# A mixture-of-experts phase in written order, its results turned by VectorE and by way of DRAM

## The chip, the cores and the metric

The kernel runs on one core of one Trainium2 chip. The metric is the device time of one execution in microseconds (us), the median of three runs. A second source is one profiled execution of the same program, whose trace gives start, duration and releaser of every instruction.

## What is computed

Eight sequences of 1024 tokens, 512 features each, pass through one layer in float32. With `xn` the layer-normalised input, the result is `x + s * silu(shared + routed)`:

```python
xn = _layernorm(x)
s = out_h @ W2 + b2                 # a gated linear recurrence over xn, projected
shared_out = _swiglu(xn, shared_gate_w, shared_up_w, shared_down_w)
topk_ids = argmax(xn @ gate_w)      # one of 32 experts for each token
xs = xn * sigmoid(topk_val)
routed_out = (silu(xs @ gate_e) * (xs @ up_e)) @ down_e   # e: the token's expert
```

Each expert has three matrices of 512x1024, 512x1024 and 1024x512, that is 2 MB each. A token goes to exactly one expert.

## The kernel before

**Two phases.** The first phase does all that is dense: normalisation, the recurrence, the shared expert and the router. It leaves in DRAM two tables of records: `rec1` holds each token's scaled input `xs`, `rec2` holds three rows for each token, its `x`, its recurrent output without the bias `b2`, and its shared output. Its instructions are issued in an order written out by hand (`tc.manual_schedule()`, closed by `order.close()`, L1397). The second phase runs over the 32 experts; here the scheduler of the framework is free to order the instructions of each engine.

**One expert.** The tokens of an expert are a chunk. Chunks are sorted by size and get fixed widths W, from 376 tokens for the first down to 224 for the last two (`WIDTHS`). A chunk of over 256 tokens has three tiles of up to 128 tokens, the others two: 20 chunks with three and 12 with two make 84 tiles. (Tokens beyond a chunk's width would go to an overflow loop at the end, L1431, which has no turn in this data.)

- `weights` (L195) loads the three matrices on SP's DMA queue into seven rotating buffers, so that a load waits for the expert that used its buffer two experts earlier.
- `gather_in` (L199) fetches `xs` on POOL's queue, 32 tokens to a DMA, so that `transpose` (L228) can turn them by VectorE in 32x32 blocks to `xsT`, with features on the partitions. The first chunk alone is fetched in whole rows and turned by TensorE.
- `gather_rest` (L218) fetches the records of `rec2`, on POOL too.
- `compute` (L252) has eight steps j. In each, TensorE multiplies gate and up (`g`, `u`, eight instructions, L272), ScalarE takes the sigmoid (L277), VectorE makes `h` (L279, L280), and TensorE multiplies the `h` of the step before by the down matrix into four PSUM tiles `acc` (L261). The trace shows each such instruction as two matmuls. So `h` of step j is wanted only after `g` and `u` of step j+1. A float32 expert is 192 pairs of weight load and matmul.
- At the end ScalarE copies the four `acc` to `yT` (L289). They hold the result with features on the partitions.
- `finish` (L291), a tile at a time and in the steps 1, 2 and 3 of the next expert, adds `b2` to the record (L297), turns `yT` back by four TensorE transposes into a PSUM tile `tb` (L300), adds the shared output (L304), takes silu with ScalarE's sigmoid (L306, L307), multiplies by the recurrent output (L308), adds `x` (L309) and scatters the rows to the output on POOL's queue (L310).

**Work between the steps.** `compute` takes a table `between` of what is issued after step j (L1412 to L1419): `finish` of the expert before, `transpose` of the next one from step 4 on, and after step 6 the weights and inputs of the expert after that. Where an instruction stands in an engine's queue is then up to the scheduler.

Of the kernel before, what the change touches and what calls it, by code (L numbers as in the profile page):

```python
# [8 lines left out]
FP = mybir.dt.float32  # L9
# [8 lines left out]
P = 128  # L18
T = 512
NT = T // P  # L20
BL = 32
# [12 lines left out]
def tile_kernel(  # L34
# [73 lines left out]
    def work(name):  # L108
        return pools["work"].tile([P, 512], FP, tag="w", name=name)
# [53 lines left out]
    def expert(where):  # L163
        e = nc.values_load(
            where, engines=[ET.SP], min_val=0, max_val=E - 1,
            skip_runtime_bounds_check_because="the numbers of experts, or a count of them, clamped",
        )
        return [w[bass.ds(e, 1)].rearrange("o a b -> (o a) b") for w in (rgate_w, rup_w, rdown_w)]

    class Chunk:  # L170
# [3 lines left out]

        def __init__(self, alloc, alloc_w, name, cols, fours, width, w_src, whole=False):
            self.whole = whole
            self.alloc, self.alloc_w, self.name, self.w_src = alloc, alloc_w, name, w_src
            self.width, self.cols, self.fours = width, cols, fours  # L180
            self.wt, self.src = [], None
            self.tiles = [
                (t, min(P, width - t * P)) for t in range(-(-width // P))
            ]
# [67 lines left out]
        def compute(self, between):  # L252


            wg, wu, wd = self.wt
            xsT, alloc, name, W = self.xsT, self.alloc, self.name, self.width
            accs = [pools["acc"].tile([P, H], FP, tag="acc", name=f"{name}_acc{m}") for m in range(KH)]

            def down(j, h):
                for m in range(KH):  # L260
                    nc.tensor.matmul(  # L261
                        accs[m][:, :W], lhsT=wd[:, j, m * P : (m + 1) * P], rhs=h[:, :W],
                        start=(j == 0), stop=(j == NI - 1),
                    )

            last = None
            for j in range(NI):
                g = work(f"{name}_g{j}")
                u = work(f"{name}_u{j}")
                for o, w in ((g, wg), (u, wu)):  # L270
                    for k in range(KH):
                        nc.tensor.matmul(  # L272
                            o[:, :W], lhsT=w[:, k, j * P : (j + 1) * P], rhs=xsT[:, k, :W],
                            start=(k == 0), stop=(k == KH - 1),
                        )
                sig = alloc([P, C], "sig", f"{name}_sig{j}")
                nc.scalar.activation(sig[:, :W], g[:, :W], AF.Sigmoid)  # L277
                h = alloc([P, C], "h", f"{name}_h{j}")
                nc.vector.tensor_tensor(sig[:, :W], sig[:, :W], g[:, :W], ALU.mult)  # L279
                nc.vector.tensor_tensor(h[:, :W], sig[:, :W], u[:, :W], ALU.mult)  # L280
                if last is not None:
                    down(*last)
                last = (j, h)
                for step in between.get(j, ()):
                    step()
            down(*last)
            self.yT = alloc([P, KH, C], "yT", f"{name}_yT")
            for m in range(KH):
                nc.scalar.copy(self.yT[:, m, :W], accs[m][:, :W])  # L289

        def finish(self, t):  # L291

            if t >= len(self.tiles):
                return
            n, col = self.tiles[t][1], self.cols(t)
            name, alloc, r = self.name, self.alloc, self.rest[t]
            nc.vector.tensor_tensor(r[:n, H : 2 * H], r[:n, H : 2 * H], b2b[:n, :], ALU.add)  # L297
            ps = work(f"{name}_tb{t}")
            for m in range(KH):
                nc.tensor.transpose(  # L300
                    ps[:n, m * P : (m + 1) * P], self.yT[:, m, t * P : t * P + n], ident
                )
            z = alloc([P, H], "z", f"{name}_z{t}")
            nc.vector.tensor_tensor(z[:n, :], ps[:n, :], r[:n, 2 * H :], ALU.add)  # L304
            s = alloc([P, H], "s", f"{name}_s{t}")
            nc.scalar.activation(s[:n, :], z[:n, :], AF.Sigmoid)  # L306
            nc.vector.tensor_tensor(z[:n, :], z[:n, :], s[:n, :], ALU.mult)  # L307
            nc.vector.tensor_tensor(z[:n, :], z[:n, :], r[:n, H : 2 * H], ALU.mult)  # L308
            nc.vector.tensor_tensor(z[:n, :], z[:n, :], r[:n, :H], ALU.add)  # L309
            nc.gpsimd.indirect_dma_start(  # L310
                out=of[:, :], out_offset=bass.IndirectOffsetOnAxis(ap=col[:n, :], axis=0),
                in_=z[:n, :], in_offset=None, bounds_check=N - 1, oob_is_err=False,
            )


    NW = 7
    turn = iter(range(3 * E))

# [2 lines left out]
        return pools["wa" if i < 4 else "wb"].tile(shape, FP, tag=f"w{i}", name=name)  # L321

    def alloc2(shape, tag, name):
        bufs = {"xs": 2 * CT, "xsT": 2, "sig": 2, "h": 3, "z": 3, "s": 2, "yT": 2, "rest": CT + 1}
        pool = pools["in" if tag in ("xs", "xsT") else "by"]
        return pool.tile(shape, FP, tag=tag, name=name, bufs=bufs[tag])

# [2 lines left out]
            alloc2, alloc_w, f"e{e}",  # L330
            lambda t, e=e: pools["idx"][:, e * CT + t : e * CT + t + 1],
            lambda t, b, e=e: pools["fours"][:, b, e * CT + t : e * CT + t + 1],
            WIDTHS[e], lambda e=e: expert(eid[0:1, e : e + 1]), e == 0,
        )
        for e in range(E)
    ]
# [44 lines left out]
    class Prep:  # L381
# [40 lines left out]
        def store(self, t):  # L422
            i = (self.c * NT + t) * P
            nc.sync.dma_start(out=xnd[i : i + P, :], in_=self.xs[t])
# [173 lines left out]
    def fetch(n):  # L598
        sum_tile(n)
        nc.sync.dma_start(  # L600
            out=sums[n].rearrange("p s k f -> p (s k f)"), in_=sdram[n % JC][:, :]
        )
# [38 lines left out]
    def bias(n, block):  # L641
        p, kind = JOBS[n % JC]
        col = "hfi".index(kind) * NJ + 2 * p + block
        return vec[:, col : col + 1]
# [749 lines left out]
    pools["work"] = ps_w  # L1394
    for t in range(CT):
        chunks[0].transpose(t)
    order.close()  # L1397
    c1.close()


    pools["acc"] = ctx.enter_context(
        tc.tile_pool(name="ps_acc", bufs=4, space=PSUM, reuse_waits="tile")
    )
    with ExitStack() as c3:
        pools["wb"] = c3.enter_context(tc.tile_pool(name="wb", bufs=1, reuse_waits="tile"))
        pools["by"] = c3.enter_context(tc.tile_pool(name="by", bufs=2, reuse_waits="tile"))
        chunks[1].weights()
        for e, chunk in enumerate(chunks):
            chunk.gather_rest()
            if e == 0:  # L1410
                chunks[1].gather_in()
            between = {j: [] for j in range(NI)}  # L1412
            for t in range(CT):
                if e:
                    between[1 + t].append(lambda t=t: chunks[e - 1].finish(t))
                if e + 1 < E:
                    between[4 + t].append(lambda t=t: chunks[e + 1].transpose(t))
            if e + 2 < E:
                between[6] += [chunks[e + 2].weights, chunks[e + 2].gather_in]  # L1419
            chunk.compute(between)  # L1420
        for t in range(CT):
            chunks[-1].finish(t)
    c2.close()


    with tc.tile_pool(name="wo", bufs=3) as wo, tc.tile_pool(name="so", bufs=3) as so:
        n = nc.values_load(  # L1427
            nov[0:1, 0:1], min_val=0, max_val=MAXOV,
            skip_runtime_bounds_check_because="a sum of at most MAXOV comparisons of counts that sum to N",
        )  # L1430
        with tc.For_i(0, n, 1) as i:  # L1431
            ci = so.tile([P, CT], I32, tag="ci", name="ci")
            nc.vector.tensor_copy(ci, pools["idx"][:, bass.ds(i * CT + E * CT, CT)])
            cf = so.tile([P, NA, CT], I32, tag="cf", name="cf")
            nc.vector.tensor_copy(cf, pools["fours"][:, :, bass.ds(i * CT + E * CT, CT)])

            def alloc(shape, tag, name):
                return so.tile(shape, FP, tag=tag, name=name)

            chunk = Chunk(  # L1440
                alloc, lambda shape, name: wo.tile(shape, FP, tag="w", name=name), "ov",
                lambda t: ci[:, t : t + 1], lambda t, b: cf[:, b, t : t + 1], C,
                lambda: expert(ovexp[0:1, bass.ds(i, 1)]),
            )
            chunk.weights()
            chunk.gather_in()
            chunk.gather_rest()
            for t in range(CT):
                chunk.transpose(t)
            chunk.compute({})  # L1450
            for t in range(CT):
                chunk.finish(t)


# [30 lines left out]
```

## Time and profile before

| | us |
|---|---|
| median of 3 runs (4343.04 to 4348.74) | 4345.41 |
| the profiled execution | 4345.11 |
| its span, first to last instruction | 4343.3 |
| first matmul of the second phase after the span's start | 2848.26 |
| end of the last expert's down matmuls, about | 4321.6 |
| TensorE busy with matmuls in between | 1467.82 of 1473.34 |
| VectorE busy there | 553.71 |
| ScalarE busy there | 203.56 |

The profile's page gives busy time by engine and groups of instructions by line. "PE" is TensorE's matmul, "PEld" its weight load, "DVE" VectorE, "ACT" ScalarE, "POOL" GpSimd, "SP" the queue that issues most DMAs. In a timeline each row has the start, the busy time and the engine of some instructions, their line and tiles, how many they are, and in brackets how long the engine stood idle before and who ended it. The recorded end of a matmul is modelled, since matmuls are pipelined: the time that one takes from its successor is read from start to start.

### The profile page before, as it was taken

The numbers are of one execution on the slowest core, as the hardware profiler recorded it, in microseconds if no ns is written. First come the engines' busy times: TensorE is split into PE (matmuls) and PEld (weight loads), VectorE is DVE, ScalarE is ACT, GpSimd is POOL, SyncE is SP. The second block draws the span as 40 slices with busy tenths as digits, with TensorE's granted clock in tenths as the row PEclk, the third lists the DMA queues.
The fourth block names the chain that finished last, engine by engine and source line by source line (L and its number), as shares of the span: only waits on it lengthen the run. The fifth ranks groups of instructions, "written<-read, shape, count | busy, mean of one in ns | idle before, by whom it ended". The sixth has DMA issues, their size and how long they took to land. (4 is left out here: it accounts for less than half of the span.)

```text
span 4343.3 us, 52479 instructions
## 1 busy us (share of the span) xinstructions
PE 4262.1 (98%) x19031; PEld 3560.0 (82%) x19031; DVE 2761.5 (64%) x3507; ACT 1661.3 (38%) x3319; POOL 1748.4 (40%) x1410
## 2 busy tenths in 40 slices
PE   8899999999999999999999999999999999999998
PEld 3488888888888888888888888866777788889998
DVE  6787877886977778778878788723334334343332
ACT  3355555555555555555555544401111111111111
POOL 4445444534453444445434536642222233332210
PEclk9999999999999999999999999999999999999999
DMA  7667676676666666766766655574555555565561
GB/s 245 204 213 225 213 222 208 207 230 206 212 213 223 219 209 209 224 202 214 223 217 214 209 187 169 183 255 165 185 185 183 177 213 201 197 230 204 205 230 63
DMA packets 459433, 889.58 MB, mean 205 GB/s; under 512 B 35167, under 2 KB 285823, under 8 KB 450980
## 3 DMA queue, kind: packets, MB, share of 16 engines
q1 hardware_dynamic: 431588, 796.22, 55.1%
q0 software_dynamic: 27584, 89.98, 6.5%
q8 instruction: 152, 2.49, 0.2%
q14 instruction: 109, 0.89, 0.1%
HBM read 787.64 MB, written 116.50 MB: 208 GB/s over the span
## 5 line engine op out<-in xcount | busy, mean ns | idle before, releaser
L694 PE MATMUL b<-t,sums 128*128 128x256 f32 x2400 | 618.9, 380 | 8.6 <-DVE t L626 6.3
L981 PE MATMUL u<-wP,s 128*128 128x256 f32 x2048 | 601.9, 381 | 2.4 <-DMA wP<-tdram 2.4
L261 PE MATMUL e_acc<-e_h,e_wd 128*128 128x296 f32 (+15 forms) x2048 | 515.4, 397 | 5.5 <-DVE e_h L280 5.5
L272 PE MATMUL e_g<-e_xsT,e_wg 128*128 128x296 f32 (+15 forms) x2048 | 518.7, 396 | 1.0 <-DVE e_xsT L242 1.0
L272 PE MATMUL e_u<-e_xsT,e_wu 128*128 128x296 f32 (+15 forms) x2048 | 518.0, 396 | 0.0
L694 PEld LDWEIGHTS b<-t,sums 128*128 128x128 f32 x2400 | 454.1, 190 | 75.4 <-issue 6.5
L212 POOL DMA_INDIRECT e_xs<-rec,fours x276 | 263.1, 953 | 553.3 <-DVE e_xsT L247 458.7
L261 PEld LDWEIGHTS e_acc<-e_h,e_wd 128*128 128x128 f32 x2048 | 390.0, 191 | 94.0 <-DVE e_h L280 6.1
L272 PEld LDWEIGHTS e_u<-e_xsT,e_wu 128*128 128x128 f32 x2048 | 389.0, 190 | 87.2
L272 PEld LDWEIGHTS e_g<-e_xsT,e_wg 128*128 128x128 f32 x2048 | 383.0, 190 | 81.9 <-DVE e_xsT L242 1.2
L981 PEld LDWEIGHTS u<-wP,s 128*128 128x128 f32 x2048 | 390.5, 191 | 57.8 <-issue 4.7
L778 DVE RECIPROCAL d<-d 128x512 f32<-128x512 f32 x128 | 427.8, 3344 | 1.6
L277 ACT ACTIVATE e_sig<-e_g 128x280 f32<-128x280 f32 (+15 forms) x256 | 102.6, 401 | 769.5 <-PE e_g L272 764.5
L279 DVE TENSOR_TENSOR e_sig<-e_sig,e_g 128x280 f32<-128x280 f32 (+15 forms) x256 | 112.1, 438 | 425.0 <-ACT e_sig L277 424.9
L762 POOL TENSOR_TENSOR f<-m,f 128x1024 f32<-128x1024 f32 x64 | 154.8, 2419 | 410.6 <-DVE m L758 321.7
L694 PE MATMUL c<-t,sums 128*128 128x256 f32 x1200 | 309.0, 380 | 6.4 <-DVE t L626 6.4
L694 PE MATMUL c<-xnT,sums 128*128 128x256 f32 x1200 | 310.1, 381 | 0.3
L694 PE MATMUL a<-xnT,nat 128*128 128x256 f32 x1200 | 309.7, 381 | 0.0
L694 PE MATMUL b<-xnT,nat 128*128 128x256 f32 x1200 | 308.0, 379 | 0.0
L694 PE MATMUL b<-t,nat 128*128 128x256 f32 x1200 | 308.0, 379 | 0.0
L694 PEld LDWEIGHTS c<-t,sums 128*128 128x128 f32 x1200 | 228.4, 190 | 37.9 <-DVE t L626 6.8
L694 PEld LDWEIGHTS c<-xnT,sums 128*128 128x128 f32 x1200 | 227.1, 190 | 37.1 <-ACT p L708 6.3
(237 smaller groups left out, 7185.8 us busy)
## 6 DMA issues: line engine op xcount, KB each, us to landing
sums<-sdram SPq DMA_DIRECT2D x300, 512.0 KB, 4.8
nat<-in_L_attn_W_dram SPq DMA_DIRECT2D x192, 512.0 KB, 4.4
wP<-tdram SPq DMA_DIRECT2D x128, 512.0 KB, 4.1
e_wg<-L_ffn_routed_gate_w_dram SPq DMA_DIRECT2D x32, 2048.0 KB, 15.5
e_wu<-n_L_ffn_routed_up_w_dram SPq DMA_DIRECT2D x32, 2048.0 KB, 8.2
e_wd<-L_ffn_routed_down_w_dram SPq DMA_DIRECT2D x32, 2048.0 KB, 13.7
nat<-L_ffn_shared_gate_w_dram SPq DMA_DIRECT2D x64, 512.0 KB, 4.6
nat<-n_L_ffn_shared_up_w_dram SPq DMA_DIRECT2D x64, 512.0 KB, 4.2
```

What stands on the lines that cost most here:

```text
L212: nc.gpsimd.indirect_dma_start(out=r[:, b, :], out_offset=None, in_=rec1.rearrange("n (a d) -> (n a) d", a=NA), in_offset=bass.IndirectOff ...
L261: nc.tensor.matmul(accs[m][:, :W], lhsT=wd[:, j, m * P : (m + 1) * P], rhs=h[:, :W], start=(j == 0), stop=(j == NI - 1),)
L272: nc.tensor.matmul(o[:, :W], lhsT=w[:, k, j * P : (j + 1) * P], rhs=xsT[:, k, :W], start=(k == 0), stop=(k == KH - 1),)
L277: nc.scalar.activation(sig[:, :W], g[:, :W], AF.Sigmoid)
L279: nc.vector.tensor_tensor(sig[:, :W], sig[:, :W], g[:, :W], ALU.mult)
L694: nc.tensor.matmul(ps, lhsT=lhs[:, k, :], rhs=rhs[:, k, :], start=(new and k == 0), stop=(k == KQ - 1),  skip_group_check=True,)
L762: nc.gpsimd.tensor_tensor(v, self.m, v, ALU.subtract)
L778: nc.vector.reciprocal(self.d[:, s, :], self.d[:, s, :])
L981: nc.tensor.matmul(ps[:, q, :], lhsT=lhs[:, q * P : (q + 1) * P], rhs=w[:, p, :],  start=(q == 0 and p == 0 and name in ("P1", "P2", "P5") ...
```

## The change

- **Written order.** The hand-written order stays open over the whole second phase (`order.close()` moves behind it), so every engine's queue holds the instructions as the code writes them.
- **Turning back.** For all experts but the last, VectorE transposes each `acc` from PSUM in 32x32 blocks straight to `yT` (four instructions for an expert, in place of ScalarE's four copies). [...] `store` writes `yT` to a DRAM buffer `ydram` with four DMAs on SP's queue, in token order and in rows of 512 bytes, and `fetch` reads it back, a DMA for each tile. The last expert (`direct`) is turned by TensorE as before, its copies split between VectorE and ScalarE.
- **Steps.** `finish` is split into `bias`, `sums` (with the sigmoid) and `finish`. For the expert before, they stand in the steps 1 to 3, 3 to 5 and 4 to 6; `store` in step 0, `fetch` in step 1. The result is written over the record, whose buffers become five in place of four.
- **Loads.** The gate matrix of the expert after next is issued in step 1, the other two in step 7; its inputs in step 2; the records of this expert in step 6 in place of ahead of it. The next expert's transposes move from steps 4 to 6 to steps 5 to 7.
- **Accumulators.** The four `acc` are made once and cleared by VectorE (four memsets), since a transpose reads whole blocks of 32 columns.

```diff
-            accs = [pools["acc"].tile(...) for m in range(KH)]
...
-            for m in range(KH):
-                nc.scalar.copy(self.yT[:, m, :W], accs[m][:, :W])
+            if self.direct:
+                self.yT = alloc([P, KH, C], "yT", f"{name}_yT")
+                for m in range(KH):
+                    if m % 2:
+                        nc.vector.tensor_copy(self.yT[:, m, :W], accs[m][:, :W])
+                    else:
+                        nc.scalar.copy(self.yT[:, m, :W], accs[m][:, :W])
+                return
+            nb = -(-W // BL)
+            self.yT = alloc([P, C // BL, KH, BL], "yT", f"{name}_yT")
+            for m in range(KH):
+                nc.vector.transpose(
+                    self.yT[:, :nb, m, :],
+                    accs[m][:, : nb * BL].rearrange("p (b c) -> p b c", c=BL),
+                )
+
+        def store(self):
+            nb = -(-self.width // BL)
+            self.y = ydram[next(yturn) % len(ydram)]
+            rows = self.y.rearrange("(b c) (a d) -> a c b d", c=BL, a=NA)
+            for a in range(NA):
+                nc.sync.dma_start(
+                    out=rows[a, :, :nb, :],
+                    in_=self.yT[a * BL : (a + 1) * BL, :nb].rearrange("p b m r -> p b (m r)"),
+                )
+
+        def fetch(self):
+            rows, self.y = self.y, []
+            for t, n in self.tiles:
+                y = self.alloc([P, H], "y", f"{self.name}_y{t}")
+                nc.sync.dma_start(out=y[:n, :], in_=rows[t * P : t * P + n, :])
+                self.y.append(y)
+
+        def sums(self, t):
...
+            z = r[:n, 2 * H :]
+            if self.direct:
+                y = work(f"{name}_tb{t}")
+                for m in range(KH):
+                    nc.tensor.transpose(...)
+                nc.vector.tensor_tensor(z, y[:n, :], z, ALU.add)
+            else:
+                zv = z.rearrange("p (m a r) -> p m a r", a=NA, r=BL)
+                y = self.y[t][:n, :].rearrange("p (a m r) -> p m a r", a=NA, r=BL)
+                nc.vector.tensor_tensor(zv, y, zv, ALU.add)
+            sg = alloc([P, H], "s", f"{name}_s{t}")
+            nc.scalar.activation(sg[:n, :], z, AF.Sigmoid)
...
-    order.close()
     c1.close()
...
+    for m in range(KH):
+        acc = pools["acc"].tile([P, H], FP, tag="acc", name=f"acc{m}")
+        nc.vector.memset(acc, 0.0)
+        accs.append(acc)
...
         chunks[1].weights()
+        chunks[1].gather_in()
         for e, chunk in enumerate(chunks):
-            chunk.gather_rest()
-            if e == 0:
-                chunks[1].gather_in()
             between = {j: [] for j in range(NI)}
+            if e:
+                before = chunks[e - 1]
+                between[0].append(before.store)
+                between[1].append(before.fetch)
+                for t in range(CT):
+                    between[1 + t].append(lambda t=t: before.bias(t))
+                    between[3 + t].append(lambda t=t: before.sums(t))
+                    between[4 + t].append(lambda t=t: before.finish(t))
+            if e + 2 < E:
+                between[1].append(lambda: chunks[e + 2].weight("g"))
+                between[2].append(chunks[e + 2].gather_in)
+            if e + 1 < E:
+                for t in range(CT):
+                    between[5 + t].append(lambda t=t: chunks[e + 1].transpose(t))
+            between[6].append(chunk.gather_rest)
+            if e + 2 < E:
+                between[7] += [lambda q=q: chunks[e + 2].weight(q) for q in "ud"]
+            if e == E - 1:
+                for t in range(CT):
+                    between[7].append(lambda t=t: chunk.bias(t))
+            chunk.compute(between)
+        for step in (chunks[-1].sums, chunks[-1].finish):
             for t in range(CT):
-                if e:
-                    between[1 + t].append(lambda t=t: chunks[e - 1].finish(t))
-                if e + 1 < E:
-                    between[4 + t].append(lambda t=t: chunks[e + 1].transpose(t))
-            if e + 2 < E:
-                between[6] += [chunks[e + 2].weights, chunks[e + 2].gather_in]
-            chunk.compute(between)
-        for t in range(CT):
-            chunks[-1].finish(t)
+                step(t)
+    order.close()
```

More of the change, by code (lines that the diff above doesn't have):

```diff
@@ L170, in tile_kernel, with __init__ @@
     class Chunk:
-        def __init__(self, alloc, alloc_w, name, cols, fours, width, w_src, whole=False):
+        def __init__(self, alloc, alloc_w, name, cols, fours, width, w_src, whole=False, direct=True):
             self.whole = whole
+            self.direct = direct
             self.alloc, self.alloc_w, self.name, self.w_src = alloc, alloc_w, name, w_src
@@ L256, in compute @@
             xsT, alloc, name, W = self.xsT, self.alloc, self.name, self.width
-            accs = [pools["acc"].tile([P, H], FP, tag="acc", name=f"{name}_acc{m}") for m in range(KH)]
             def down(j, h):
@@ L286, in compute @@
             down(*last)
-            self.yT = alloc([P, KH, C], "yT", f"{name}_yT")
-            for m in range(KH):
-                nc.scalar.copy(self.yT[:, m, :W], accs[m][:, :W])
+            if self.direct:
[6 more added lines that the diff above has]
+                return
@@ new lines, in fetch @@
+        def fetch(self):
[5 more added lines that the diff above has]
+        def sums(self, t):
+            if t >= len(self.tiles):
+                return
+            n = self.tiles[t][1]
+            name, alloc, r = self.name, self.alloc, self.rest[t]
+            z = r[:n, 2 * H :]
+            if self.direct:
+                y = work(f"{name}_tb{t}")
+                for m in range(KH):
+                    nc.tensor.transpose(
+                        y[:n, m * P : (m + 1) * P], self.yT[:, m, t * P : t * P + n], ident
+                    )
+                nc.vector.tensor_tensor(z, y[:n, :], z, ALU.add)
[5 more added lines that the diff above has]
+            nc.scalar.activation(sg[:n, :], z, AF.Sigmoid)
+            self.gate = getattr(self, "gate", {})
+            self.gate[t] = z, sg
@@ L291, in finish, with bias @@
+        def bias(self, t):
+            if t < len(self.tiles):
+                n, r = self.tiles[t][1], self.rest[t]
+                nc.vector.tensor_tensor(r[:n, H : 2 * H], r[:n, H : 2 * H], b2b[:n, :], ALU.add)
         def finish(self, t):
@@ L294, in finish @@
                 return
[L295 to L298, printed above, removed]
-            for m in range(KH):
[L300 to L309, printed above, removed]
+            n, col, r = self.tiles[t][1], self.cols(t), self.rest[t]
+            z, sg = self.gate[t]
+            nc.vector.tensor_tensor(z, z, sg[:n, :], ALU.mult)
+            nc.vector.tensor_tensor(z, z, r[:n, H : 2 * H], ALU.mult)
+            nc.vector.tensor_tensor(z, z, r[:n, :H], ALU.add)
             nc.gpsimd.indirect_dma_start(
                 out=of[:, :], out_offset=bass.IndirectOffsetOnAxis(ap=col[:n, :], axis=0),
-                in_=z[:n, :], in_offset=None, bounds_check=N - 1, oob_is_err=False,
+                in_=z, in_offset=None, bounds_check=N - 1, oob_is_err=False,
             )
+    accs = []
+    ydram = [dram.tile([C, H], FP, name=f"ydram{q}") for q in range(3)]
+    yturn = iter(range(E))
     NW = 7
@@ L323, in alloc2 @@
     def alloc2(shape, tag, name):
-        bufs = {"xs": 2 * CT, "xsT": 2, "sig": 2, "h": 3, "z": 3, "s": 2, "yT": 2, "rest": CT + 1}
+        bufs = {"xs": 2 * CT, "xsT": 2, "sig": 2, "h": 3, "y": 3, "s": 2, "yT": 2, "rest": CT + 2}
         pool = pools["in" if tag in ("xs", "xsT") else "by"]
@@ L332, in tile_kernel @@
             lambda t, b, e=e: pools["fours"][:, b, e * CT + t : e * CT + t + 1],
-            WIDTHS[e], lambda e=e: expert(eid[0:1, e : e + 1]), e == 0,
+            WIDTHS[e], lambda e=e: expert(eid[0:1, e : e + 1]), e == 0, e == E - 1,
         )
@@ L1451, in tile_kernel @@
             for t in range(CT):
+                chunk.bias(t)
+                chunk.sums(t)
                 chunk.finish(t)
```

## The prediction, made before the result was known

> **What bounds the kernel now.** I read the busy time by stage first, then the timelines of one boundary between experts and of the start of the second phase, then groups and DMA issues. By stage (columns: stretch, its length, then busy us and instructions of PE, PEld, DVE, ACT, POOL, granted clock, DMA share, GB/s), the second phase:
>
> ```profile
> 2848.26:4321.60 1473.34, 1467.82 (x6472) 1198.99 (x6473) 553.71 (x1005) 203.56 (x465) 418.61 (x430) 1.00 0.55 193
> ```
>
> TensorE is the bound of the phase: 5.5 us idle in 1473. VectorE is busy 38%, ScalarE 14%. So a TensorE instruction less is time less, and VectorE has room. One boundary inside the phase, expert 13 to which expert 12's results belong (timeline, all engines):
>
> ```profile
> 3535.69 2.05 PE L261 MATMUL e_acc<-e_h,e_wd 128*128 128x280 f32 x8
> ...
> 3537.57 0.60 PE L300 MATMUL e_tb<-ident,e_yT 128*128 128x128 f32 x4
> ...
> 3538.01 2.05 PE L272 MATMUL e_g<-e_xsT,e_wg 128*128 128x280 f32 x8
> 3538.21 0.69 DVE L304 TENSOR_TENSOR e_z<-e_tb,e_rest 128x512 f32<-128x512 f32 x1 [1.88 <-PE e_tb L300]
> ```
>
> The eight matmuls take 3537.57 - 3535.69 = 1.88 us from start to start, the four transposes 3538.01 - 3537.57 = 0.44, with no gap. The narrow tiles show the same 0.44 (24 tokens: 3549.77 to 3550.21). The one hole is in the first expert:
>
> ```profile
> 2863.53 2.69 PE L272 MATMUL e_u<-e_xsT,e_wu 128*128 128x376 f32 x8
> ...
> 2866.12 0.69 DVE L297 TENSOR_TENSOR e_rest<-e_rest,b2b 128x512 f32<-128x512 f32 x1 [11.90 <-DMA e_rest<-rec,idx]
> ...
> 2869.88 0.69 DVE L297 TENSOR_TENSOR e_rest<-e_rest,b2b 128x512 f32<-128x512 f32 x1 [3.07 <-DMA e_rest<-rec,idx]
> ...
> 2871.74 5.38 PE L261 MATMUL e_acc<-e_h,e_wd 128*128 128x376 f32 x8 [5.52 <-DVE e_h L280]
> ```
>
> The scheduler put bias additions ahead of an `h`; VectorE waits for their records (11.90 and 3.07 us), `h` comes late, TensorE idles 5.5 us and runs the next eight matmuls at half speed (5.38 against 2.69). Its full price: expert 1 (width 352) goes from 2917.77 to 2975.89, less three groups of 0.44, over 192 matmuls 295.8 ns each; expert 2 (336, to 3031.45) 282.5. That is 13.3 ns for 16 columns, so 315.8 for width 376: 60.6 us, and expert 0 took 2917.77 - 2848.26 = 69.5. The hole costs 8.9.
>
> [...] The landings (from issue, last column) agree:
>
> ```profile
> e_wg<-L_ffn_routed_gate_w_dram SPq DMA_DIRECT2D x32, 2048.0 KB, 15.5
> e_wu<-n_L_ffn_routed_up_w_dram SPq DMA_DIRECT2D x32, 2048.0 KB, 8.2
> e_wd<-L_ffn_routed_down_w_dram SPq DMA_DIRECT2D x32, 2048.0 KB, 13.7
> ...
> xr<-xnd SPq DMA_DIRECT2D x60, 256.0 KB, 4.7
> ```
>
> Issued within 6 us at each boundary (u, d, g), they land one after the other.
>
> **Part by part.**
>
> *TensorE's transposes go.*
>
> ```profile
> L300 PE MATMUL e_tb<-ident,e_yT 128*128 128x128 f32 (+4 forms) x336 | 50.5, 273 | 0.0
> ```
>
> 336 instructions are 84 tiles. The last expert's two tiles stay (and run after the matmuls); 82 x 0.44 = 36.1 us leave the engine that bounds. This is the surest term.
>
> *VectorE's transposes come.* Four for an expert, of 224 to 384 columns, from PSUM. The trace has them from SBUF: 1.08 us for 512 columns, 0.36 for 128 (L247), so about 0.66 for 288. PSUM as a source costs nothing in this trace (L304 with PSUM 689 ns, L307 without 688). Bounds: 0.36 and 1.1. They start as each `acc` is done. The next expert's `down(0)`, which overwrites `acc`, comes 16 instructions (32 matmuls) later: 7.5 us at width 280 (235.8 ns each), 6.1 at 224. Four times 0.66 is 2.6, behind it only a pair of products of 0.8. Hidden at either bound; uncovered from about 1.6 us each. ScalarE loses 4 x 0.39 us an expert, which was hidden too.
>
> *The hole goes.* In the built program VectorE's queue in expert 0 holds four memsets (about 0.65 each, as a copy of this size at L242), the products, and the next transposes only in step 5; no bias stands ahead of an `h`. The memsets run from 2848.1, where three transposes ran before (2848.12 to 2851.77), and the first product came at 2851.70. Records for expert 0 are gathered about 2870 and wanted in expert 1. Gain 8.9; bounds 0 (something else is late there) and 8.9.
>
> *Store and fetch.* SP issues store when `yT` is written, about 1 us into the expert, then waits for it before fetch; behind this wait stands the gate load of the expert after next, not wanted for over 60 us. Take width 232 (expert 29, start 4208.75): u issued at 4204.24, d at 4205.81, so d lands 10.8 us into the expert. Store follows: 1024 rows of 512 bytes over 16 engines. The queue's mean packet is 89 ns (55.1% of 16 x 4343 us over 431588 packets), 512-byte reads are recorded at 27 ns: 1.7 to 5.7 us. Fetch 4.7. So y is there at 17 to 21. VectorE comes to `sums` after h3, at about 16, and may wait. Then 0.69 + sigmoid 0.63 + the next sigmoid 0.36 + products 0.8 = 2.5 us until h4, which TensorE wants in `down(4)`, 25.1 us into the expert (16 + 4 x 24 + 16 matmuls of 195.8 ns). So y must be there by 22.5. At width 280 it is 15 to 21 against 27.5. Covered by 2 to 12 us; cost nothing. The added bytes (about 0.6 MB each way, beside 9 MB an expert) go into an idle half: DMA share 0.55.
>
> *POOL, ScalarE.* Scatters come three steps later, behind the gathers of inputs, and the records' gathers behind them: at width 232 issued after `finish` of step 5, 28 us into the expert, landed (5.1 us) by about 35, wanted in the next expert's step 1, at 44. POOL's waits hold up nothing else. ScalarE's sigmoid of `sums` stands ahead of the sigmoid of the next step; counted above. Nothing.
>
> *VectorE in the fullest step* (5, three tiles): products 0.9, `finish` 2.05, `sums` 0.69, transpose 1.08: 4.7 of 5.3 us and more. Covered, just.
>
> *The tail.*
>
> ```profile
> 4322.59 1.28 DVE L304 TENSOR_TENSOR e_z<-e_tb,e_rest 128x512 f32<-128x512 f32 x2 [3.41 <-PE e_tb L300]
> ...
> 4327.40 1.19 POOL L310 DMA_INDIRECT out_dram<-e_z,idx  x1 [24.52 <-DVE e_z L309]
> 4331.15 0.94 POOL L310 DMA_INDIRECT out_dram<-e_z,idx  x1 [2.56 <-issue]
> ```
>
> Before, the two tiles go in turn, so the first scatter follows seven operations; in written order it follows five: 2 x 0.64 = 1.3 us earlier, and the second scatter follows the first's landing. Gain 1.3, bounds 0 and 2.
>
> Sum: 4345.1 - 36.1 - 8.9 - 1.3 = 4298.8 for the profiled execution; the median lies 0.3 above it: **4299**.
>
> **Rivals.**
>
> *The hole moves* (a wait at the start of the phase for inputs or clearing takes its place): 4299 + 8.9 = 4308. For it: POOL now begins the next inputs after its last addition of the first phase. Against: they are wanted 30 us later. 9%.
>
> *Small waits at many steps.* The order by hand leaves VectorE little slack in step 5; 0.4 us in each of 31 experts is 12: 4311. Against: `h` has a whole step to spare. 9%.
>
> *Late y.* Store in 512-byte rows is slow, `sums` holds h4, TensorE stalls in each expert. Room for store: 22.5 - 10.8 - 4.7 = 7.0 us at width 232 (64 rows an engine), 27.5 - 10.1 - 4.7 = 12.7 at width 280 (72). With t a row, 12 narrow and 19 wide experts lose 12 (64t - 7.0) + 19 (72t - 12.7), where positive; this eats the gain of 46 from t = 169 ns. The trace shows no such write; at the 234 ns of the largest gather packets in its records the loss is 175: 4474, slower. For it: nothing here writes rows so short. Against: reads of that size at 27 ns. 7%.
>
> *The transposes don't leave the path*: the build shows none between the matmuls but for the last expert; no rival.
>
> **How the numbers follow.** Likeliest 75%: 4294 to 4305. With the hole moved and small waits, 18%, up to 4314. Slower 7%. The range 4292 to 4314 leaves out some 15 in 100. A measurement of this kernel tells about 0.2%, 9 us, from no change. Faster 0.91, same 0.02, slower 0.07.
>
> **What would show it.** Right: no `tb` matmuls but eight; an expert of width 280 lasting 45.3 us in place of 46.6 (192 x 235.8 ns); expert 0 at 60.6; VectorE's transposes near 0.66; waits of `sums` for DMA without waits of TensorE. Wrong: TensorE waiting for `h` in step 4 or 5 (late y), or for VectorE at `down(0)` (slow transposes).

## The result, and the profile after

| | before | after |
|---|---|---|
| median of 4 runs each, us | 4345.42 (4343.04 to 4348.74) | 4301.36 (4299.96 to 4303.85) |
| the profiled execution; its span | 4345.11; 4343.3 | 4299.96; 4298.2 |
| first matmul of the second phase | 2848.26 | 2847.85 |
| expert 0 (width 376), from its first `g` to that of the next | 69.51 | 60.74 |
| expert 1 (352) | 58.12 | 56.80 |
| an expert of width 280; of width 232 | 46.60; 38.48 | 45.28; 37.60 |
| end of the span after TensorE's last down matmul | 21.7 | 21.8 |

The ratio is 0.9901, 95% interval 0.9888 to 0.9913. The spans differ by 45.1 us: 0.4 from the first phase, which has the same instructions and jitters; 8.8 in expert 0; 36.1 for 82 groups of four transposes at 0.44; and -0.1 at the end.

The stage (stretch, length, busy us and instructions of PE, PEld, DVE, ACT, POOL, then granted clock, DMA share, GB/s), from the first `g` to the last down matmul of the kernel after:

```profile
2847.85:4276.60 1428.75, 1428.75 (x6145) 1169.47 (x6145) 621.13 (x1133) 151.47 (x340) 428.12 (x437) 1.00 0.65 225
```

TensorE has no idle time left in 1429 us; before, it had 5.5. VectorE has 67 us more work, ScalarE 52 less. TensorE's waits from 2840 us to the end of the span are only these (waiting engine and tile, who ended the wait, us in all, times, longest), the first at the start of the phase, the second in the tail:

```profile
PE e_g L272 <- DVE e_xsT L243: 1.0, 1, 1.0
PE e_tb L332 <- DVE e_yT L291: 0.5, 1, 0.5
```

The boundary where expert 12 ends and expert 13 begins, and expert 13's first down projection, which the prediction shows for the kernel before (timeline of the kernel after):

```profile
3499.38 3.94 PE L261 MATMUL acc<-e_h,e_wd 128*128 128x280 f32 x16
...
3501.94 1.90 DVE L299 STREAM_TRANSPOSE e_yT<-acc 128x288 f32<-128x288 f32 x4 [1.59 <-PE acc L261]
...
3503.16 2.05 PE L272 MATMUL e_g<-e_xsT,e_wg 128*128 128x280 f32 x8
...
3503.87 10.27 SPq L310 DMA_DIRECT2D ydram<-e_yT  x4
...
3510.70 2.05 PE L261 MATMUL acc<-e_h,e_wd 128*128 128x280 f32 x8
...
3512.59 2.05 PE L272 MATMUL e_g<-e_xsT,e_wg 128*128 128x280 f32 x8
...
3520.81 1.29 SPq L319 DMA_DIRECT2D e_y<-ydram  x3
...
3523.47 0.69 DVE L339 TENSOR_TENSOR e_rest<-e_y,e_rest 128x512 f32<-128x512 f32 x1 [0.80 <-DMA e_y<-ydram]
```

At the boundary the last two down projections and the next `g` follow one another as before (16 matmuls in 3503.16 - 3499.38 = 3.78). Where four `tb` stood, between expert 13's first down projection and the `g` after it, there is nothing left: 3512.59 - 3510.70 = 1.89 for the eight matmuls, where it was 1.88 and 0.44. VectorE's transposes begin 1.2 us before expert 13 does. The four stores are issued over 10.3 us; I had them issued at once. Why the blocks that VectorE turned go by DRAM is read from the diff: each store takes 32 partitions of `yT`, which hold 128 of the 512 features of each token, and a row of `ydram` brings the four parts together. `y` is fetched 17.7 us into the expert and used 20.3 us into it; VectorE waits 0.80 for it, TensorE not at all.

Expert 0, where the hole was (the kernel after):

```profile
2847.91 2.10 DVE L1457 MEMSET acc<- 128x512 f32 x4
...
2858.06 2.69 PE L261 MATMUL acc<-e_h,e_wd 128*128 128x376 f32 x8
...
2863.12 2.69 PE L272 MATMUL e_u<-e_xsT,e_wu 128*128 128x376 f32 x8
...
2865.64 2.69 PE L261 MATMUL acc<-e_h,e_wd 128*128 128x376 f32 x8
```

The down projection follows `u` by 2865.64 - 2863.12 = 2.52 for eight matmuls, 315 ns each, where the prediction's estimate for this width was 315.8; behind the hole of the kernel before, eight took some 627 ns each.

VectorE's two new groups (busy us, mean ns | idle before them, and who ended it):

```profile
L299 DVE STREAM_TRANSPOSE e_yT<-acc 128x288 f32<-128x288 f32 (+5 forms) x124 | 58.1, 485 | 50.7 <-PE acc L261 48.3 <-issue 1.9
L339 DVE TENSOR_TENSOR e_rest<-e_y,e_rest 128x512 f32<-128x512 f32 (+9 forms) x82 | 56.1, 684 | 22.0 <-DMA e_y<-ydram 22.0
```

And the landings (KB each, median us from issue to the arrival of the data):

```profile
e_wg<-L_ffn_routed_gate_w_dram SPq DMA_DIRECT2D x32, 2048.0 KB, 8.5
e_wu<-n_L_ffn_routed_up_w_dram SPq DMA_DIRECT2D x32, 2048.0 KB, 11.6
e_wd<-L_ffn_routed_down_w_dram SPq DMA_DIRECT2D x32, 2048.0 KB, 19.3
e_y<-ydram SPq DMA_DIRECT2D x53, 256.0 KB, 3.0
ydram<-e_yT SPq DMA_DIRECT2D x40, 144.0 KB, 9.7
e_rest<-rec,idx POOLq DMA_INDIRECT x84, 10.5
```

The up and down matrices (`u` and `d`) land later than before (8.2 and 13.7); the gate matrix, now issued by itself, sooner (15.5). It is not the stores that delay `d`: the first experiment below has none, and there it takes nearly as long:

```profile
e_wd<-L_ffn_routed_down_w_dram SPq DMA_DIRECT2D x32, 2048.0 KB, 18.5
```

What has moved to this place in both kernels is the gathers of the records (`e_rest`), which landed after 5.1 us before. The packets of the trace (the pieces that the DMA engines move, each with its start and size) show it at expert 13: records from 0.7 us before its first `g` to 9.3 after, `d` from 2.2 to 15.1, the rows of the stores from 12.8 to 17.2. In the kernel before, `d` was through at 10.1. That the gathers delay `d` fits, but no run moved them alone. A stored row of 512 bytes takes 27 ns (mean of 35968 packets).

### The profile page after: what moved, and what is told of

It is laid out like the page before. It is cut to its first block, busy times and chain, and to the rows that moved or that the text cites. A ratio compares the mean times of both kernels' runs of the same rounds, so it can differ in the third digit from the quotient of the medians.

```text
span 4298.2 us, 52089 instructions
## 1 busy us (share of the span) xinstructions
PE 4221.4 (98%) x18703; PEld 3534.2 (82%) x18703; DVE 2830.7 (66%) x3637; ACT 1607.1 (37%) x3193; POOL 1751.5 (41%) x1410
## 4 chain that ended last, share of the span: by engine, by line
PE 91%; DVE 4%; POOL 2%; issue 2%; DMA 1%; ACT 0%; SPq 0%; POOLq 0%; DVEq 0%; ACTq 0%
PE b L746 23%; PE u L1033 17%; PE c L746 11%; PE e_g L272 11%; PE e_u L272 11%; PE acc L261 11%; PE a L746 6%; DVE d L830 1%; POOL i L814 0%; PE b L706 0%; DMA wP<-tdram 0%; PE lgp L519 0%; POOL tab L1280 0%; POOL i L823 0%; POOL f L823 0%
## 5 line engine op out<-in xcount | busy, mean ns | idle before, releaser
L261 PE MATMUL acc<-e_h,e_wd 128*128 128x296 f32 (+15 forms) x2048 | 513.0, 396 | 0.0
L261 PEld LDWEIGHTS acc<-e_h,e_wd 128*128 128x128 f32 x2048 | 389.8, 190 | 86.3
L359 POOL DMA_INDIRECT out_dram<-e_rest,idx x84 | 93.4, 1112 | 804.1 <-DVE e_rest L358 801.0
L280 DVE TENSOR_TENSOR e_h<-e_sig,e_u 128x280 f32<-128x280 f32 (+15 forms) x256 | 113.2, 442 | 245.7 <-PE e_u L272 245.4
## 6 DMA issues: line engine op xcount, KB each, us to landing
e_wd<-L_ffn_routed_down_w_dram SPq DMA_DIRECT2D x32, 2048.0 KB, 19.3
```

The source lines that it names most:

```text
L261: nc.tensor.matmul(accs[m][:, :W], lhsT=wd[:, j, m * P : (m + 1) * P], rhs=h[:, :W], start=(j == 0), stop=(j == NI - 1),)
L359: nc.gpsimd.indirect_dma_start(out=of[:, :], out_offset=bass.IndirectOffsetOnAxis(ap=col[:n, :], axis=0), in_=z, in_offset=None, bounds_ch ...
```

## The experiments

Each run stood beside runs of the kernel before on the same chip; their time is given with it. Two questions were to be told apart: are the two gains independent, as the sum had it, and how much cover was left for the transposes and for `y`, that is, how much longer could they take before TensorE waits for them?

The losses by step below are worked out from starts in the traces: the first down matmul of each step, counted from its expert's first `g`, less the same in the kernel after. `down(4)` is the down projection of step 4, which needs `h4`, the `h` of that step.

**The order alone** (the kernel after with all experts turned by TensorE, and no store and fetch; the new steps, loads and gathers stay):

```diff
-            WIDTHS[e], lambda e=e: expert(eid[0:1, e : e + 1]), e == 0, e == E - 1,
+            WIDTHS[e], lambda e=e: expert(eid[0:1, e : e + 1]), e == 0,
...
-                between[0].append(before.store)
-                between[1].append(before.fetch)
```

> The changed kernel with all experts turned back by TensorE (no store, no fetch), in written order. Theory (the gain is 36.1 us of TensorE transposes and 8.9 us of the hole): only the hole goes, so 4345.4 - 8.9 = 4336, and expert 0 lasts 60.7 us while an expert of width 280 keeps 46.6. Rival (the written order itself speeds up every expert): well below 4336, towards 4301.

Measured: 4336.64 (17 runs, 4333.61 to 4338.66) against 4344.15, ratio 0.9982 (0.9975 to 0.9989). Expert 0 lasts 60.74, an expert of width 280 46.60 as before. The written order, with the steps that go with it, is worth the hole and nothing else.

**The hole alone** (the kernel before; `b2` is left out of the gate for the first two experts, so no bias addition can wait there):

```diff
-            nc.vector.tensor_tensor(r[:n, H : 2 * H], r[:n, H : 2 * H], b2b[:n, :], ALU.add)
+            if name not in ("e0", "e1"):
+                nc.vector.tensor_tensor(r[:n, H : 2 * H], r[:n, H : 2 * H], b2b[:n, :], ALU.add)
```

> The kernel before, with the addition of b2 left out for the first two experts (their output lacks that bias), so that no VectorE instruction waits for records ahead of a product; all else unchanged. Theory: the hole's cause is this wait, expert 0 falls from 69.5 to 60.7 us, 4345.4 - 8.9 = 4336.5. Rival (the late h has another cause, DMA traffic or POOL at the start): 4345.

Measured: 4337.2 (18 runs, 4333.52 to 4339.98), ratio 0.9983 (0.9976 to 0.9990), expert 0 at 60.74. So the bias additions that waited for their records were the hole, shown from both sides.

**The turning with the scheduler's order** (the kernel after, but the second phase left to the scheduler; the new places of the loads and gathers stay):

```diff
     c1.close()
+    order.close()
...
-    order.close()
     c2.close()
```

> The changed kernel with the hand-written order closed where it was before: VectorE turns, store and fetch are there, the scheduler orders the second phase. If the TensorE transposes were all: 4345.4 - 36.1 = 4309 with a hole as before in expert 0. But in the built program the gate load stands between store and fetch on SP, so y lands behind 2 MB (some 5 us later, 22 to 25 us into the expert), and VectorE's first sum stands ahead of the third product h3, which TensorE wants at 20.4 us (width 232) to 24.5 us (width 280). By that the late-y mechanism costs about 1 us in each of 19 wide experts and 2.7 in 11 narrow ones, 50 us in all: 4360, with TensorE waiting for h in step 4. The two differ by 50 us.

Measured: 4446.84 (4 runs, 4436.82 to 4452.77), ratio 1.0229 (1.0211 to 1.0246): 2.3% slower than before, and slower than either theory. Its waits, longest of those that matter:

```profile
DVE e_rest L348 <- DMA e_rest<-rec,idx: 329.6, 79, 19.2
...
PE acc L261 <- DVE e_h L280: 114.3, 26, 14.5
```

and one place of it, the end of an expert of width 280 (the sixteen matmuls behind the wait, of `acc` and the `g` of the next expert, take 3488.44 - 3482.87 = 5.57 us from start to start, where sixteen took 3.78 in the kernel after):

```profile
3478.35 0.69 DVE L348 TENSOR_TENSOR e_rest<-e_rest,b2b 128x512 f32<-128x512 f32 x1 [4.07 <-DMA e_rest<-rec,idx]
...
3481.22 0.69 DVE L348 TENSOR_TENSOR e_rest<-e_rest,b2b 128x512 f32<-128x512 f32 x1 [2.18 <-DMA e_rest<-rec,idx]
3481.83 0.44 DVE L279 TENSOR_TENSOR e_sig<-e_sig,e_g 128x280 f32<-128x280 f32 x1
3482.37 0.45 DVE L280 TENSOR_TENSOR e_h<-e_sig,e_u 128x280 f32<-128x280 f32 x1
...
3482.87 2.74 PE L261 MATMUL acc<-e_h,e_wd 128*128 128x280 f32 x8 [2.55 <-DVE e_h L280]
3485.40 3.20 PE L272 MATMUL e_g<-e_xsT,e_wg 128*128 128x280 f32 x8
...
3488.44 2.05 PE L272 MATMUL e_u<-e_xsT,e_wu 128*128 128x280 f32 x8
```

This is the hole of expert 0 again, now at the end of many experts: bias additions ahead of the products, their records not there yet. The turning is not alone here. In the kernel before, the records of this expert (expert 11) are gathered 14.2 to 27.9 us into it and the additions start at 19.3 to 33.0; here the gathers, moved to step 6 for the written order, start at 32.8 to 38.1, and the additions that wait for them at 36.5 to 44.5, among the last products. So the later gathers have a part in this loss, and no run here turns by VectorE with the gathers where they were. In the profiled execution (span 4451.0) 17.3 us are lost in expert 0; of experts 1 to 30, 120 at the last step (100 waiting, 20 at a slower clock behind the wait) and some 14 ahead of the first down projection. Neither of my theories for this run named that.

**The same without the bias.** A new theory, then: bias additions are the whole loss. The same kernel, without them (the gate lacks `b2`):

```diff
         def bias(self, t):
-            if t < len(self.tiles):
+            if t < len(self.tiles) and self.name == "ov":
```

> Turning alone (the order of the second phase left to the scheduler), and b2 left out of the gate for all experts, so that no bias addition stands ahead of an h. If the 138 us over the forecast for turning alone are bias additions that wait for their records ahead of products (expert 0: 17, experts 7 to 30: 0.3 to 12.6 each), they go: 4300 to 4320, an expert of width 280 at 45.3 to 46, TensorE without waits for h beyond some 10 us. If they are results that come late from DRAM, or other work that the scheduler places ahead of the products, at least half of them stay: 4370 to 4440, with waits of VectorE for y or for other transfers in place of those for records.

Measured: 4311.6 (one run; before 4349.67). TensorE's waits:

```profile
PE acc L261 <- DVE e_h L280: 5.0, 1, 5.0
PE e_g L272 <- DVE e_xsT L243: 4.4, 1, 4.4
```

All experts from 1 to 30 have the lengths of the kernel after, to 0.01 us. What is left lies in expert 0 (69.76, 9.0 over) and ahead of it, and is of another kind (see the next run). VectorE's other 995 instructions in these experts stand in the same order in both traces, and the gathers are as late, so it is the additions and not another order. The theory holds: with no bias addition in the way, the scheduler's order loses nothing in these experts, and late `y` alone costs nothing.

**The transposes three times.** How much cover do they have?

```diff
-            for m in range(KH):
+            for m in list(range(KH)) * 3:
                 nc.vector.transpose(
```

> The kernel after, with each of VectorE's four transposes of an expert done three times. 12 x 0.485 = 5.8 us on average, about 5.2 at width 232, and a pair of products of 0.8 behind them: 6.6 of 7.5 us at width 280, 6.0 of 6.3 at 232. Theory (they are hidden until about 1.6 us each, here 1.5): no change, 4300 to 4306, with waits of TensorE for h of under 10 us in all. Rival (they stand on the path, since the accumulators come free late): 8 x 0.485 = 3.9 us in each of 31 experts, 120 us, 4421.

Measured: 4341.81 (one run; before 4349.67), neither expectation. 18.7 us are lost in expert 0, though its instructions there are those of the kernel after:

```profile
2873.74 0.55 DVE L280 TENSOR_TENSOR e_h<-e_sig,e_u 128x376 f32<-128x376 f32 x1 [14.40 <-remote]
2873.83 0.48 ACT L277 ACTIVATE e_sig<-e_g 128x376 f32<-128x376 f32 x1 [15.07 <-remote]
2874.34 4.91 PE L261 MATMUL acc<-e_h,e_wd 128*128 128x376 f32 x8 [14.59 <-DVE e_h L280]
```

VectorE and ScalarE both stand until the same moment, though their inputs are ready from 2859.4 on (the product of VectorE that ends there is the last of them); "remote" is what the profile says where it sees no releaser in this core. A further 23 us are lost in 19 later experts. Inconclusive.

**Five times** (the same edit with 5), on the same chip:

> The kernel after, with each of VectorE's four transposes of an expert done five times. 20 x 0.485 = 9.7 us, with the products 10.5, against 7.5 us of cover at width 280: 3.0 us uncovered; at width 232 20 x 0.43 + 0.8 - 6.3 = 3.1. Theory: 31 x 3.0 = 93 us, 4394; between 4380 and 4420, and up to 4500 if the idle time halves TensorE's clock as the hole of expert 0 did. Rival (there is more cover than counted): under 4320. Rival (no cover): 16 x 0.485 x 31 = 240, 4540.

Measured: 4387.41 (one run; before 4349.67), with 18.8 us lost in expert 0 and the same unexplained rows. That 4394 had been expected is no evidence: in experts 12 to 18 three and five transposes lost the same 0.7 to 1.6 us ahead of the first down projection, so it was not their number. All four runs of this group, the one without the bias too, had such rows on ScalarE and VectorE, and they ran on another chip than the runs before them. Hence a control and a repeat.

**The control:** the kernel after, unchanged.

> The kernel after, unchanged, as a control for the runs beside it. In the three runs v3, v5 and s4 expert 0 lasted 79.2 to 79.5 us in place of 60.7, with ScalarE and VectorE both idle until the same moment for nothing that the profile shows, although the first expert's instructions are the same as in the kernel after. If that belongs to the edits: 4300 to 4303 here, expert 0 at 60.74. If it belongs to the chip they ran on: here too, should that chip come again, 4319 to 4322; on another chip none, and then the run of five transposes beside this one has none either.

Measured: 4300.63 (4 runs, 4299.99 to 4301.64; before 4342.26), ratio 0.9904 (0.9887 to 0.9920), every expert as in the first profile.

**Five times, beside the control:**

> Each of VectorE's transposes five times, once more, beside the kernel after. In the first run experts 10 to 30 lost 0.4 to 8 us each ahead of the first down projection, and three and five transposes lost the same in experts 12 to 18 (0.7 to 1.6 us). If the transposes' own time does it (20 x 0.40 + 0.8 = 8.8 us at width 280, against 7.5 and the 1.2 us that the transposes start ahead of the next expert: 8.7), the wide experts lose under 0.5 us and the narrow ones, whose transposes are shorter too, the same: 4300 to 4320, expert 0 at 60.74. If the formula with 0.485 us each and no early start holds: 4394. If the losses of the first run come with any edit here: 4385 to 4390 as before, with expert 0 at 79.

Measured: 4308.81 (one run; span 4307.1), expert 0 at 60.74, no unexplained rows. The group, and TensorE's wait for `h`:

```profile
L299 DVE STREAM_TRANSPOSE e_yT<-acc 128x288 f32<-128x288 f32 (+5 forms) x620 | 239.8, 449 | 50.6 <-PE acc L261 48.3 <-issue 1.9
```

```profile
PE acc L261 <- DVE e_h L280: 2.1, 7, 0.6
```

240 us of transposes cost 7.6 us. At width 280 they lie exactly at the edge:

```profile
3503.87 7.73 DVE L299 STREAM_TRANSPOSE e_yT<-acc 128x288 f32<-128x288 f32 x20 [1.59 <-PE acc L261]
3505.09 2.05 PE L272 MATMUL e_g<-e_xsT,e_wg 128*128 128x280 f32 x8
...
3512.04 0.45 DVE L280 TENSOR_TENSOR e_h<-e_sig,e_u 128x280 f32<-128x280 f32 x1
...
3512.63 2.06 PE L261 MATMUL acc<-e_h,e_wd 128*128 128x280 f32 x8
```

They start 1.22 us ahead of the expert, take 7.73 / 20 = 0.39 each, and `h` is done at 3512.49, when the down projection would start unhindered at 3505.09 + 7.54 = 3512.63. The cover is 1.9 us for each of the four places.

**The store twice** (a store to another array ahead of the true one):

```diff
-            rows = self.y.rearrange("(b c) (a d) -> a c b d", c=BL, a=NA)
-            for a in range(NA):
+            for to in [yextra] * 1 + [self.y]:
+              rows = to.rearrange("(b c) (a d) -> a c b d", c=BL, a=NA)
+              for a in range(NA):
...
```

> The changed kernel with the results stored twice, first to a spare DRAM tile, then to the true one, so y lands later by one store, about 4 us. Now y is read at 16.5 to 17.2 us (width 232) and 20.0 (width 264), and must be there by 22.5 and 25.9 for TensorE not to wait. Theory: VectorE waits longer, TensorE not: 4300 to 4302, an expert of width 280 at 45.3 us. Rival (there is no slack left): each expert longer by up to 4 us, 4400.

Measured: 4302.04 (one run, span 4300.3). TensorE's experts keep their lengths; VectorE's wait for `y` triples from 22.0:

```profile
DVE e_rest L340 <- DMA e_y<-ydram: 63.8, 28, 3.9
```

**The store four times** (`[yextra] * 3`):

> The kernel after, with three stores to another array ahead of the true one. One such store moved the fetch by 2 us; in it each further four issues took 5.5 us, so the fetch is issued at about 30 us into an expert of width 280 and 26 at 232, y lands 3 us later, and 2.5 us of sums, sigmoid and products follow: 35.5 against 30.2, 31.5 against 25.1, when TensorE wants h4. Theory (late y is the rival's mechanism, and the kernel after lies 5 to 10 us before its point): TensorE waits for h in step 4, 5 to 6 us an expert, 150 to 190 us in all: 4450 to 4490, up to 4560 with a halved clock. Rival (y is never on TensorE's path, or the stores overlap): under 4330.

Measured: 4412.76 (one run; before 4349.67), in the group with the unexplained rows: 18.5 us lost in expert 0, 79.6 at `down(4)` and behind it, some 12 elsewhere. So once more:

> Three stores to another array ahead of the true one, once more, since the first run stood beside runs with stalls that the profile does not explain (18.5 us of it in expert 0, some 12 us ahead of the first, second and third down projection). In its trace TensorE lost 79.6 us ahead of down(4) and the matmuls behind it, in experts 6 to 30: 58.9 waiting, 20.7 at a slower clock. Theory (these 79.6 us are the late y and nothing else): 4301 + 80 = 4381 here, 4370 to 4390, expert 0 at 60.74, all of the loss at down(4). If the unexplained stalls made them: under 4340.

Measured: 4397.43 (one run; before 4343.86), expert 0 at 60.74, none of those rows. In experts 1 to 30 all but 1 us of the loss is at `down(4)`: 66.1 waiting and 27.9 at a slower clock behind it. That is more than the 80 expected. `y` is not used later for it (in the experts of two tiles 27.4 us into them on average, in both runs). In the first run experts 16 to 29 had already lost 9.5 us ahead of `down(4)`, so that late `y` had less to cost there; and some 7 us of the difference are matmuls at the slower clock. The waits and one place (an expert of width 280 that starts at 3514.24):

```profile
DVE e_rest L340 <- DMA e_y<-ydram: 283.3, 29, 11.9
...
PE acc L261 <- DVE e_h L280: 62.6, 24, 5.6
```

```profile
3540.57 1.29 SPq L320 DMA_DIRECT2D e_y<-ydram  x3
...
3543.18 0.69 DVE L340 TENSOR_TENSOR e_rest<-e_y,e_rest 128x512 f32<-128x512 f32 x1 [9.43 <-DMA e_y<-ydram]
...
3545.46 0.45 DVE L280 TENSOR_TENSOR e_h<-e_sig,e_u 128x280 f32<-128x280 f32 x1
...
3545.96 2.15 PE L261 MATMUL acc<-e_h,e_wd 128*128 128x280 f32 x8 [1.38 <-DVE e_h L280]
```

`y` is used at 28.9 us, and the down projection that wants `h4` starts at 31.7 where the kernel after has it at 30.2. This is the rival "late y" with its place and chain, and TensorE stalls behind it as described. It takes three more stores to get there.

**The tail** (the last expert's records gathered in step 3, its bias additions in step 6):

```diff
-            between[6].append(chunk.gather_rest)
+            between[6 if e < E - 1 else 3].append(chunk.gather_rest)
...
-                    between[7].append(lambda t=t: chunk.bias(t))
+                    between[6].append(lambda t=t: chunk.bias(t))
```

> The kernel after, with the last expert's records gathered in step 3 in place of 6 and both bias additions in step 6. Theory of the tail (the bias addition that waited 1.4 us for its records held VectorE's two copies, so TensorE's last transposes and the first sum came 0.5 us later than before): the copies start when the accumulators are done, the first sum about 1.0 us after the last down projection in place of 1.5, and the span ends some 21.2 us after it in place of 21.76. In the time 0.5 us, which is under what the measurement tells: 4300 to 4302 where the kernel after has 4301. Rival (the tail is set by the scatters alone): 21.76 as before.

Measured: 4302.17 (4 runs, 4299.28 to 4303.60; before 4342.26), not told apart from the control's 4300.63. The tail of the kernel after, and then of this one:

```profile
4276.21 0.69 DVE L348 TENSOR_TENSOR e_rest<-e_rest,b2b 96x512 f32<-96x512 f32 x1 [1.41 <-DMA e_rest<-rec,idx]
...
4277.92 1.28 DVE L335 TENSOR_TENSOR e_rest<-e_tb,e_rest 128x512 f32<-128x512 f32 x2 [0.42 <-PE e_tb L332]
...
4281.78 1.22 POOL L359 DMA_INDIRECT out_dram<-e_rest,idx  x1 [11.03 <-DVE e_rest L358]
...
4286.09 0.96 POOL L359 DMA_INDIRECT out_dram<-e_rest,idx  x1 [3.09 <-DMA out_dram<-e_rest,idx]
```

```profile
4280.85 1.28 DVE L335 TENSOR_TENSOR e_rest<-e_tb,e_rest 128x512 f32<-128x512 f32 x2 [0.42 <-PE e_tb L332]
...
4284.70 1.19 POOL L359 DMA_INDIRECT out_dram<-e_rest,idx  x1 [13.10 <-DVE e_rest L358]
...
4289.71 0.94 POOL L359 DMA_INDIRECT out_dram<-e_rest,idx  x1 [3.81 <-issue]
```

Counted from TensorE's first `tb` after the last down matmul (4321.62 before, 4276.43 after, 4279.84 here):

| | before | after | this run |
|---|---|---|---|
| first sum | 0.97 | 1.49 | 1.01 |
| first scatter | 5.78 | 5.35 | 4.86 |
| second scatter | 9.53 | 9.66 | 9.87 |
| end of the span | 21.7 | 21.8 | 22.0 |

The bias addition did delay the sums by 0.5 us, and taking its wait away moves the first scatter up; the second scatter, and with it the end, does not follow. The trace records when the first scatter lands, counted in the same way: 8.80 after, 8.83 in the control, 9.09 here, and the second is issued 0.8 to 0.9 later each time. So the second does follow the first's landing, but a first scatter issued sooner does not land sooner. The rival of this run holds.

## Why the prediction was right

Forecast 4299, measured 4301.36, and the profiled execution 4299.96 where the sum gave 4298.8. Of a forecast gain of 46.3 us in that execution 45.1 came, 0.4 of it by luck (the first phase was shorter by so much); what is missing is the term of the tail.

- *TensorE's transposes go*: 36.1 forecast, 36.1 found, and an expert of width 280 at 45.28 where 45.3 was named. With the order alone as the base the turning gives 4336.64 - 4301.36 = 35.3.
- *VectorE's transposes come*: at no cost, as said. The size was off on the safe side: 0.485 us each where 0.66 was estimated, and the cover is 1.9 us for each of the four at width 280 and not 1.6, since the first `acc` are done 1.2 us before the next expert starts.
- *The hole goes*: 8.8 of 8.9; nothing took its place, and two runs show its cause.
- *Store and fetch*: cost nothing, as said. At width 232 the fetch is issued at 13.8 to 14.5 us into the expert, where the forecast has 12.5 to 16.5, and `y` is used at 16.5 to 17.2. At width 280 two errors cancel: the fetch is issued at 17.6 to 17.8, later than the 10 to 16 that the forecast implies, and it takes 3.0 us in place of 4.7; `y` is used at 20.3 to 20.8, inside the forecast of 15 to 21. The fetch is late because `d` is: the forecast took `d`'s landing from the kernel before (10.1 us into the expert), and now its packets run to 15.1. The slow issue of the stores is not the reason, for the last is issued by 11.0 and the rows move from 12.8 on, behind `d`. That the store would follow `d` was my estimate, for in the trace before only the weights are seen to land one after the other (`u`, `d`, `g`: 8.2, 13.7 and 15.5 us from issue); at expert 13 of this trace it did for the most part, with rows from 12.8 to 17.2 and `d` to 15.1. The limits of 27.5 and 22.5 were exact: in the repeat with four stores `y` is used at 27.8, 28.5 and 28.9 at width 280, and TensorE waits 0.4, 1.1 and 1.5 us more; at 27.6 and 28.2 at width 232, and it waits 5.2 and 5.7.
- *Late y* as a rival: its price was asked in ns for a row, with the gain gone at 169, and a row takes 27, the value that the prediction held against it. Its mechanism and place were right, as four stores show. At width 232 the kernel after lies some 5 us from the point, at 280 some 7.
- *The tail*: the one term that failed, 1.3 us. The first scatter follows five operations in place of seven, as said, and is issued 0.4 sooner (the late sums took 0.5). The second follows its landing, as said too. What failed is the step between, that the landing comes sooner by as much as the issue: issued at 5.35, 5.11 and 4.86 us (after, control, tail's own run), the first scatter lands at 8.80, 8.83 and 9.09. Why it does not land sooner stays open.
- *The hole moves, small waits*: neither came. Yet an order that lets VectorE wait ahead of `h` is what the run with the scheduler's order shows at its full size: 145 us more than the kernel after. The prediction took the two parts as a plain sum. They do add up (8.8 and 36.1) as long as the order is by hand; with the scheduler's order, and the gathers where the written order wants them, the turning comes with a loss of 103 us, and without bias additions it does not.

## What to carry to other kernels

When work leaves the bounding engine, what it moves to has to be priced by the next deadline behind it in that engine's queue, counted from when its input is ready; here 1.9 us of room for 0.4 us of work. An instruction that may wait for a DMA is not to be placed ahead of one that the bounding engine needs: here VectorE waited for records (11.90 and 3.07 us) with the products of an `h` behind it, and two such additions cost 8.8 us in one expert, and some 145 us when the scheduler did it at most boundaries, with gathers that had been moved for another order. A gain at a step that is followed by a wait for something else (here the first scatter, issued 0.49 us sooner and landed 0.29 later) is not a gain until that wait is priced.

## What the runs showed of the hardware that was not expected

- **The stores behind loads were slow to be issued.** In the kernel after SP took 10.3 us for the four stores in expert 13 (3503.87), 2.9 in expert 1 and 2.7 in the last expert, which has no load ahead of them; three fetches took 1.3. `d`'s packets, ahead of the stores in the queue, run to 15.1 us in expert 13 and to 6.5 in expert 1. That the load ahead sets the pace of the issue is my guess from these times; no run varied that alone. In the run with four times the stores the first four were issued 0.7 to 9.8 us into an expert of width 280, the next not before 15.6, and all twelve of these within 6.8.
- **Half speed behind short pauses.** In the repeat with four stores, pauses (from the recorded end of a matmul to the next start) of up to 2.0 us were followed by matmuls at full speed, pauses of 2.10, 2.33 and 2.33 by some 3.4 us of matmuls at half speed (at width 264 from 222 to 440 ns), one of 2.65 not, and all eleven over 2.7. In the first run with five transposes one of 1.98 was followed by them and one of 3.42 was not. So in these two runs the length of a pause between 1.98 and 3.42 us did not tell whether half speed followed, and a slowed one cost 1.5 to 3 us more. What decides it was not shown.
- **Two engines that stop together.** On one chip all four kernels lost 9 to 19 us in expert 0, VectorE and ScalarE idle with their inputs ready, in three of them for some 14 us and until the same moment, in the one without the bias for 8 and 11. The DMA engines were full (share 0.99 to 1.02 from 2846 to 2876 us), but so they are in the kernel after (1.00). Two of the four were run again on two other chips and had none of it; no run shows the kernel after itself on the first chip beside them. No packet of an instruction queue lies in that stretch. The cause is open.
